# The beginning of layer 3 in a four-layer graph kernel: four groups of nodes between the last chunks of hop 2, residual and factor in one product, roots from bits

## The chip, the cores and the metric

The kernel runs on 1 core of one Trainium2 chip, as one launch. The metric is the device time in microseconds (us), as a median of runs. The profile is of one further execution of the program. In its lines PE is TensorE (PEld its weight loads), DVE is VectorE, ACT is ScalarE, POOL is GpSimd, and SPq is the queue of SyncE, which here issues nearly all transfers. A line such as L386 is line 386 of the kernel as it is before the change.

## The reference, cut to what matters

Four layers work on x (3327 nodes of 64 features) and one adjacency matrix adj (3327 x 3327); after each, the layer's input is added and a layernorm taken. Layers 2 and 3 are touched here:

```python
def _L2_gnn_ref(user_embs, adj, W):
    x = user_embs
    for k in range(2):                     # two hops
        agg = adj @ x
        x = jnp.tanh(jnp.concatenate([agg, x], axis=1) @ W[k])
    return x
def _L3_gnn_ref(input, adj, weight, bias):
    support = input @ weight
    mask = (adj != 0).astype(support.dtype)
    rank = jnp.cumsum(mask, axis=1)
    deg = rank[:, -1:]
    k = jnp.minimum(deg, 100.0)
    pos = rank - (deg - k)
    w = mask * jnp.where(pos > 0, 0.5 ** (k - pos), 0.0)
    return w @ support + bias
...
x = _layernorm(x + _L2_gnn_ref(x, adj, L2_gnn_W), axis=-1)
x = _layernorm(x + _L3_gnn_ref(x, adj, L3_gnn_weight, L3_gnn_bias), axis=-1)
```

Layer 3 gives each neighbour a weight that halves with every further neighbour that comes after it in its row. So it needs a count along the row, and products with weights that the count makes.

## The kernel before, in words

**Tiling.** The nodes are padded to 3328, 26 blocks of 128. The matrix comes transposed, so a block of 128 rows of `in_adjT` holds all edges that come from 128 nodes: 128 partitions x 3328 values, 1664 KB. A feature-major tensor such as `hT` is 128 x 1664: the 64 features of the first half of the nodes on 64 partitions, those of the second half on the other 64. It is cut into 4 chunks of 416 columns (`CPH`, `CW`).

**A hop of layer 2** (`for k in range(2)` in `layers`) adds 26 blocks into four accumulators in PSUM, one per chunk, each a tile of its own (`acc`, pool `l2a`). `add(c, jb)` (L386) does chunk c of block jb: two float32 products, one for each half, side by side on 64 columns of TensorE each. `top` and `bottom` (L344, L374, L377) multiply the node features with the two halves of W. Six blocks stay in SBUF: 25 to 22 (tiles `kept`, pool `early`) and 21, 20 (pool `late`). Six more are left over from the hop before (`ready`). Hop 2 streams the other 14 through two buffers `bt` and four buffers `at` (L204): a load is issued when the block that was in its buffer has been added. In what follows these 14 are s0 to s13, and the 26 blocks of hop 2 stand at places 0 to 25. Before the change places 0 to 5 are the left-over blocks, places 6, 11, 16 and 21 are the kept blocks 25 to 22, and the streamed blocks stand between them, s12 and s13 at places 22 and 23. The kept blocks 20 and 21 are last, chunk by chunk, so that each chunk can go through its tanh (L453, on ACT) while the next is added:

```python
                for c in range(CPH) if k == 0 else reversed(range(CPH)):
                    for jb in stay[-2:]:
                        add(c, jb, jb == stay[-1])
                    nc.scalar.activation(nxt[:, c * CW : (c + 1) * CW], acc[c], AF.Tanh)
```

After the second streamed block of hop 2, six masks (L326, DVE) are made from the six kept blocks, for the first six steps of layer 3.

**The beginning of layer 3** follows hop 2. `residual` turns h back to node-major and centers it in one product (L529), adds x2, squares and sums (L534, L537, L538). `scaled` takes roots with ACT's Sqrt and a Newton step (L231 to L238) and scales (L546). `turned` transposes x3 (L553, L557), and `factor` multiplies it by the weight matrix (L563) and splits the product into three bfloat16 parts (L569, L570, L571 and, on POOL, L572). These work on groups of 1, 4, 4 and 4 column blocks. Between them stand the first counting steps, `counts(0)` to `counts(2)`.

**The main loop** does 52 steps, 26 blocks for each half of the target nodes. Step q does for c = 0, 1: `advance` (L468; two products with `rest`, two with `tri`, into the count tiles `cnt`) and `products` of the step three before (L614; and every third step a group of 12 smaller ones, L627). Before a count tile can move on it must be read: `read` (L484 on ACT for c = 0, L482 on DVE for c = 1) turns its bits into weights `w`. DVE also makes the mask of the step three ahead from a half block `ah`, of which four are in flight (L324). Between the halves, `sums_out` (L643 on ACT, L644 on DVE) takes the first half's sums out of PSUM, and `half_out` (L653 to L679) does bias, residual and layernorm.

**What sets the order.** Every engine works through its own queue in order. TensorE's queue is in the order of the code throughout. In the two hops and the main loop DVE's and ACT's queues are too (`manual_schedule`); in the beginning of layer 3 a scheduler orders these two. Waits between engines are put in by the framework, by tiles.

Of the kernel before, what the change touches and what calls it, by code (L numbers as in the profile page):

```python
# [10 lines left out]
F32 = mybir.dt.float32  # L11
# [55 lines left out]
STEP = float(2**7)  # L67


@with_exitstack  # L70
def kernel(
# [65 lines left out]
    w3_dg = const.tile([P, P], F32, name="w3_dg")  # L137
# [39 lines left out]
    center = const.tile([P, P], F32, name="center")  # L177
# [120 lines left out]
    def layers(ctx, x2, kept, ready, ahead_ctx, strm):  # L298
# [52 lines left out]
        x3 = xpool.tile([P, NB, D], F32, tag="x", name="x3")  # L351
        hT = cols.tile([P, HALF], F32, tag="hT", name="hT_0")
        with tc.tile_pool(
            name="l2p", bufs=2, space=PSUM, reuse_waits="tile"
        ) as l2p, tc.tile_pool(
            name="l2a", bufs=CPH, space=PSUM, reuse_waits="tile"
        ) as l2a, tc.manual_schedule(
            engines={mybir.EngineType.DVE, mybir.EngineType.Activation}
        ):
            for k in range(2):  # L360
                hw = lj
                nxt = cols.tile([P, HALF], F32, tag="hT", name=f"hT_{k + 1}")
                acc = [l2a.tile([P, CW], F32, tag="acc", name=f"acc2_{k}_{c}") for c in range(CPH)]
# [30 lines left out]

                stay = list(kept)
                others = [jb for jb in range(NB) if jb not in kept and jb not in ready]
                share = -(-len(others) // (len(stay) - 2))
                order = list(ready)
                for i, jb in enumerate(stay[:-2]):
                    order += [jb] + others[i * share : (i + 1) * share]  # L400
                blocks = {**ready, **kept}

                if k == 0:
# [14 lines left out]
                    for c in range(CPH):  # L418
                        bottom(c)

# [29 lines left out]
                for c in range(CPH) if k == 0 else reversed(range(CPH)):  # L450
                    for jb in stay[-2:]:
                        add(c, jb, jb == stay[-1])
                    nc.scalar.activation(nxt[:, c * CW : (c + 1) * CW], acc[c], AF.Tanh)  # L453

# [18 lines left out]
        def read(q):  # L473
            if q >= len(steps):
                return
            h, jb = steps[q]
            for c in range(2):
                w = l3w.tile(
                    [P, 2, CW], BF16, tag=f"w{c}", bufs=LEAD + GROUP + 2, name=f"w_{h}_{jb}_{c}"
                )  # L480
                if c:
                    nc.vector.tensor_scalar(w.bitcast(I16), cnt[c], 0.0, None, ALU.max)  # L482
                else:
                    nc.scalar.activation(w.bitcast(I16), cnt[c], AF.Relu)  # L484
                ws[q, c] = w
# [10 lines left out]
        def rsqrt_of(v, w):  # L496

            nc.vector.tensor_scalar(v, v, 1.0 / D, LN_EPS, ALU.mult, ALU.add)
            return rsqrt(v, "ln", w)

        def spread(v, n):
# [8 lines left out]
        xT = cols.tile([P, HALF], F32, tag="hT", name="xT_3")  # L510
        s12 = l3n.tile([P, NB, 2, D], BF16, name="s12")
        s3 = l3n.tile([P, NB, D], BF16, name="s3")
        rr = lj
        l3w = ctx.enter_context(tc.tile_pool(name="l3w", bufs=2, reuse_waits="tile"))
        l3c = ctx.enter_context(
            tc.tile_pool(name="l3c", bufs=1, space=PSUM, reuse_waits="tile")
        )
        cnt = [l3c.tile([P, 2, 512], F32, name=f"cnt_{c}")[:, :, :CW] for c in range(2)]

        with tc.tile_pool(name="l3t", bufs=4, space=PSUM, reuse_waits="tile") as l3t:  # L520

            def ps(name):
                return l3t.tile([P, 4 * P], F32, tag="ps", name=name)

            def residual(g, n):

                pr = ps(f"pr_h2_{g}")
                for c in range(n):
                    nc.tensor.matmul(  # L529
                        pr[:, c * P : (c + 1) * P], hT[:, (g + c) * P : (g + c + 1) * P], center,  # L530
                        start=True, stop=True,
                    )
                sl = slice(2 * g, 2 * (g + n))
                nc.vector.tensor_tensor(  # L534
                    hid[:, sl], pr[:, : n * P].rearrange("p (n d) -> p n d", d=D), x2[:, sl], ALU.add
                )
                nc.scalar.activation(sq[:, sl], hid[:, sl], AF.Square)  # L537
                nc.vector.tensor_reduce(var[:, sl], sq[:, sl], axis=AX.X, op=ALU.add)  # L538

            def scaled(part):  # L540
                sl = slice(2 * part[-1][0], 2 * (part[0][0] + part[0][1]))
                r = rsqrt_of(var[:, sl], sl.stop - sl.start)
                for g, n in part:
                    s = slice(2 * g, 2 * (g + n))
                    o = s.start - sl.start
                    nc.vector.tensor_tensor(  # L546
                        x3[:, s], hid[:, s], spread(r[:, o : o + 2 * n], 2 * n), ALU.mult
                    )

            def turned(g, n, copy):  # L550
                pt = ps(f"pt_x3_{g}")
                for c in range(n):
                    nc.tensor.transpose(  # L553
                        pt[:, c * P : (c + 1) * P],
                        by_half(x3)[:, g + c].rearrange("p h d -> p (h d)"), ident,
                    )
                copy(xT[:, g * P : (g + n) * P], pt[:, : n * P])  # L557

            def factor(g, n):

                pn = ps(f"pn_l3_{g}")
                for c in range(n):
                    nc.tensor.matmul(  # L563
                        pn[:, c * P : (c + 1) * P], xT[:, (g + c) * P : (g + c + 1) * P], w3_dg,
                        start=True, stop=True,
                    )
                pn = pn[:, : n * P].rearrange("p (n d) -> p n d", d=D)
                sl = slice(2 * g, 2 * (g + n))
                nc.scalar.copy(s12[:, sl, 0, :], pn)  # L569
                nc.vector.tensor_tensor(rr[:, sl], pn, s12[:, sl, 0, :], ALU.subtract)  # L570
                nc.scalar.copy(s12[:, sl, 1, :], rr[:, sl])  # L571
                nc.gpsimd.tensor_tensor(s3[:, sl], rr[:, sl], s12[:, sl, 1, :], ALU.subtract)  # L572

            def counts(q):
                read(q)
                for c in range(2):
                    advance(c, q)

            last, second = fours[:1:-1], fours[1::-1]
            for g, n in last + second:  # L580
                residual(g, n)
            scaled(last)
            scaled(second)
            for c in range(2):
                count(c, tri, 0, True)
            counts(0)
            turned(*last[0], nc.scalar.copy)
            turned(*last[1], nc.vector.tensor_copy)
            counts(1)
            factor(*last[0])  # L590
            factor(*last[1])
            turned(*second[0], nc.scalar.copy)
            turned(*second[1], nc.vector.tensor_copy)
            counts(2)
            factor(*second[0])
            factor(*second[1])

# [85 lines left out]
        with tc.manual_schedule(engines={mybir.EngineType.DVE, mybir.EngineType.Activation}):  # L683
            for q in range(LEAD, len(steps) + LEAD + 1):
                read(q)
                masks(q + AHEAD)
                p = q - LEAD if q < NB + LEAD else q - LEAD - 1
                for c in range(2):
                    if q < len(steps):
                        advance(c, q)  # L690
                    if q != NB + LEAD:
                        products(p, c)
                if q == NB + LEAD - 1:
                    accT = sums_out(0)
                if q == NB + LEAD:
                    first_out = half_out(0, accT)
                if first_out is not None:
                    next(first_out, None)
# [17 lines left out]
    with tc.tile_pool(name="l1", bufs=1) as l1:  # L716
# [811 lines left out]

        n_below = nc.values_load(flag[0:1, 0:1])
        with tc.If(n_below == 0) as norms:  # L1530
            with ExitStack() as arm:
                x2 = xpool.tile([P, NB, D], F32, tag="x", name="x2")
                with tc.tile_pool(name="n1m", bufs=1) as n1m:
                    mT = n1m.tile([P, HALF], F32, name="mT")
                    sq_e = n1m.tile([P, 12, D], F32, name="sq_e")
                    t_e = n1m.tile([P, 12], F32, name="t_e")

                    xm = x2.rearrange("p n d -> p (n d)")[:, : 3 * CW]
                    near_sphere(mT, xm, sq_e, t_e)
                    blocks = blocks_ahead(arm)  # L1540
                    near_end(mT, xm, sq_e, t_e, x2)
                layers(x2, *blocks)
        with norms.Else():
            with ExitStack() as arm:
                x1 = xc
                x2 = xpool.tile([P, NB, D], F32, tag="x", name="x2_any")
# [6 lines left out]
                layers(x2, *blocks)  # L1553
# [31 lines left out]
```

## Time and profile before

| | us |
|---|---|
| median of 3 runs | 577.2 |
| the runs | 579.83, 574.63, 577.20 |
| the profiled execution, whole | 574.9 |
| its span in the profile | 573.2 |
| PE, DVE, ACT, POOL busy in the span | 529.3, 361.6, 275.0, 216.4 |
| mean granted TensorE clock | 0.985 |
| transfers | 145.26 MB, 253 GB/s over the span |

The profiled execution is 1.7 us longer than its span. Layer 3 with its beginning takes the last 165 us of the span. PE's busy time says that PE is occupied, not that it is at its peak: matmuls overlap, and their ends are modelled. A line of the timeline gives the start, the time taken, engine, source line, operation, tiles, the number of merged instructions, and in brackets how long the engine was idle before it and what ended that.

### The profile page before, as it was taken

To read this page: it belongs to the slowest core of one execution; us is meant where nothing else is said; L and a number is where in the kernel's file an instruction comes from. 1 tells how busy PE (TensorE), PEld (TensorE's weight loads), DVE (VectorE), ACT (ScalarE), POOL (GpSimd) and SP (SyncE) were. 2 spreads that over 40 slices of the span, in tenths; PEclk is the share of its full clock that TensorE was granted. 3 is DMA by queue.
4 is the path that set the end of the run, shared out by engine and by line. 5 is a ranking of instruction groups with operands and counts; after the bars stand their busy time and mean duration, and the time that the engine had idled before them with its cause. 6 is when DMAs were issued, how large, how long until landed. Compare 5 with 4: busy or idle time off the path is not lost.

```text
span 573.2 us, 7492 instructions
## 1 busy us (share of the span) xinstructions
PE 529.3 (92%) x2864; PEld 226.3 (39%) x2864; DVE 361.6 (63%) x510; ACT 275.0 (48%) x327; POOL 216.4 (38%) x134
## 2 busy tenths in 40 slices
PE   8899989999999999699999999999879999899992
PEld 5522222222222224254444444433455555555542
DVE  7899999999999998920000010300487787698733
ACT  4999999998999997330000100000453333333320
POOL 3799999999999998100000000000020000000000
PEclk9999999999999999989999999999999999999996
DMA  8977675650766653999999049996618995689701
GB/s 294 369 257 223 214 231 193 236 180 3 237 210 215 232 180 123 396 428 423 426 426 396 5 176 424 373 406 289 236 64 274 330 339 192 235 266 355 247 1 35
DMA packets 34020, 145.26 MB, mean 253 GB/s; under 512 B 10269, under 2 KB 11959, under 8 KB 28855
## 3 DMA queue, kind: packets, MB, share of 16 engines
q1 hardware_dynamic: 32295, 144.27, 68.4%
q10 hardware_dynamic: 1680, 0.43, 0.3%
q8 instruction: 24, 0.39, 0.3%
q14 instruction: 21, 0.17, 0.1%
HBM read 143.23 MB, written 0.87 MB: 251 GB/s over the span
## 4 chain that ended last, share of the span: by engine, by line
PE 63%; DVE 20%; ACT 9%; issue 3%; DMA 3%; DVEq 0%; POOL 0%; POOLq 0%; ACTq 0%
PE acc L386 24%; PE pq L910 12%; DVE v L931 12%; PE cnt L468 11%; PE acc L614 5%; ACT sg L886 3%; PE acc L627 3%; ACT pq L923 2%; DVE a L922 2%; DMA at_l<-in_adjT 2%; DVE w L482 2%; PE pn_l L344 1%; PE pr_o L653 1%; PE acc L377 1%; DVE mask L326 1%
## 5 line engine op out<-in xcount | busy, mean ns | idle before, releaser
L897 POOL TENSOR_TENSOR u<-sg,at 128x832 f32<-128x832 f32 x88 | 169.8, 1957 | 3.2 <-ACT sg L886 2.7
L910 PE MATMUL pq<-riT,ljT 64*128 64x416 f32 x416 | 100.3, 560 | 15.2 <-DVE v L931 6.3
L922 DVE SCALAR_TENSOR_TENSOR a<-pq,dl,u 128x832 f32<-128x832 f32 x104 | 111.9, 1077 | 3.0 <-PE pq L910 2.9
L923 ACT ACTIVATE pq<-pq,al,gas 128x832 f32<-128x832 f32 x104 | 104.9, 1010 | 15.2 <-DVE a L922 14.2
L931 DVE SCALAR_TENSOR_TENSOR v<-pq,a 128x832 f32<-128x832 f32 x104 | 105.7, 1016 | 1.1 <-ACT pq L923 0.8
L943 PE MATMUL acc<-v,xv 128*64 128x416 f32 x416 | 95.4, 538 | 0.1
L386 PE MATMUL acc<-at_l,lj 128*64 128x416 f32 x480 | 86.5, 514 | 1.0 <-DMA at_l<-in_adjT 1.0
L886 ACT ACTIVATE sg<-lb,rb 128x1664 f32<-128x1664 f32 (+1 forms) x53 | 87.3, 1647 | 0.1
L484 ACT ACTIVATE w<-cnt 128x832 int16<-128x832 f32 x52 | 44.8, 862 | 72.9 <-PE cnt L468 72.8
L453 ACT ACTIVATE hT<-acc 128x416 f32<-128x416 f32 x8 | 4.1, 517 | 149.4 <-PE acc L386 149.4
L572 POOL TENSOR_TENSOR s<-lj,s 128x512 bf16<-128x512 f32 (+1 forms) x4 | 3.9, 977 | 182.8 <-ACT s L571 182.8
L482 DVE TENSOR_SCALAR w<-cnt 128x832 int16<-128x832 f32 x52 | 53.2, 1024 | 26.3 <-PE cnt L468 25.0
L910 PEld LDWEIGHTS pq<-riT,ljT 64*128 64x128 f32 x416 | 31.6, 185 | 88.3 <-DVE v L931 83.0
L374 DVE COPY lj<-pn_l 128x384 f32<-128x384 f32 (+2 forms) x8 | 4.3, 542 | 86.7 <-PE pn_l L344 86.7
L468 PE MATMUL cnt<-mask,rest 128*128 128x416 bf16 x200 | 51.7, 340 | 3.3 <-ACT w L484 2.5
L386 PEld LDWEIGHTS acc<-at_l,lj 128*64 128x64 f32 x480 | 34.1, 138 | 50.6 <-issue 47.9
L468 PE MATMUL cnt<-mask,tri 128*128 128x416 bf16 x208 | 53.4, 339 | 0.1
L614 PE MATMUL acc<-w,s 128*128 128x416 bf16 x208 | 52.3, 340 | 0.8 <-DVE lj L570 0.8
L943 PEld LDWEIGHTS acc<-v,xv 128*64 128x64 f32 x416 | 20.6, 135 | 61.0 <-issue 57.7
L326 DVE TENSOR_SCALAR mask<-ah 128x1664 bf16<-128x1664 f32 x42 | 43.4, 1033 | 0.0
L386 PE MATMUL acc<-kept,lj 128*64 128x416 f32 x192 | 35.2, 513 | 0.0
L897 POOL TENSOR_TENSOR u<-sg,kept 128x832 f32<-128x832 f32 x16 | 30.9, 1965 | 3.8 <-ACT sg L886 3.8
(266 smaller groups left out, 391.8 us busy)
## 6 DMA issues: line engine op xcount, KB each, us to landing
at_l<-in_adjT SPq DMA_DIRECT2D x26, 1664.0 KB, 12.3
at<-in_adjT SPq DMA_DIRECT2D x44, 832.0 KB, 4.9
ah<-in_adjT SPq DMA_DIRECT2D x42, 832.0 KB, 6.6
bt_l<-in_adjT SPq DMA_DIRECT2D x8, 1664.0 KB, 11.1
kept<-in_adjT SPq DMA_DIRECT2D x6, 1664.0 KB, 8.7
lb<-lf_rows SPq DMA_DIRECT2D x2, 384.0 KB, 4.5
ljT<-ljT SPq DMA_DIRECT2D x4, 128.0 KB, 6.4
out<-hid SPq DMA_DIRECT2D x2, 256.0 KB, 5.8
```

The source lines that it names most:

```text
L326: nc.vector.tensor_scalar(mask[q], at, 0.0, None, ALU.not_equal)
L386: nc.tensor.matmul(acc[c][h * D : (h + 1) * D, :], hw[:, slot(jb), :], blocks[jb][:, o : o + CW], start=c not in begun, stop=last, skip_gr ...
L468: nc.tensor.matmul(cnt[c][:, e, :], mat, mask[q][:, of], start=start, stop=(mat is tri), skip_group_check=True,)
L482: nc.vector.tensor_scalar(w.bitcast(I16), cnt[c], 0.0, None, ALU.max)
L614: nc.tensor.matmul(acc[h, c][:, e, :], s12[:, slot(jb)].rearrange("p t d -> p (t d)"), ws[q, c][:, e, :], start=first, stop=last,)
L886: nc.scalar.activation(sg[:, :, of], lbs[:, :, of], AF.Sigmoid, bias=rb[:, sl : sl + 1])
L897: nc.gpsimd.tensor_tensor(u, sg[:, :, of], at[:, :, of], ALU.mult)
L910: nc.tensor.matmul(pq[:, h, :], ljT[h != jb // NBH][rows, of], riT[rows, ch * CW : (ch + 1) * CW], start=True, stop=True,)
L922: stt(a_s[t], pqs[t], dl[:, one], us.pop(t), op0=ALU.add, op1=ALU.mult)
L923: nc.scalar.activation(pqs[t], pqs[t], AF.Square, bias=al[:, one], scale=gas[:, one])
L931: stt(w, pqs.pop(t), CUBIC_REST, a_s.pop(t), op0=ALU.add, op1=ALU.mult)
L943: nc.tensor.matmul(accs[cp, ci][h * D : (h + 1) * D, :], xv[:, slot(jb), :], w[:, h, :], start=(jb == order[0]), stop=(jb == order[-1]),)
```

## The change

- The accumulators of the hops are no longer four tiles but the two count tiles of layer 3: chunks 0 and 1 are the two halves of the tile `cnt_0`, chunks 2 and 3 those of `cnt_1`.
- x2 is transposed into the memory of an earlier tensor and stays (`x2T`). So h + x2 is added feature-major (`with_x2`), chunk by chunk, after the tanh.
- At the start of hop 1 one product and one copy on ACT (`pw_3`) put center x weight beside `center`. With both as one 128 x 256 operand (`both_m`) one product gives the centered residual and its product with the weights (`finish`); scaling both by the root comes after.
- Roots are made on DVE alone, from the bits of the number (`roots`, nine instructions), not with ACT's Sqrt.
- The nodes are taken in four groups A, B, C, E of 3, 3, 3 and 4 column blocks, and the work on them stands between the last chunks of hop 2, in an order written out for PE, DVE and ACT.
- Hop 2 keeps three blocks for its end (24, 23, 22), not two (20, 21); 20 and 21 come at places 6 and 12, 25 at place 18, s12 and s13 at places 21 and 22.
- Between the halves, the reads of the next step now stand ahead of `sums_out`.

```diff
+        x2T = x3.rearrange("p n d -> p (n d)")
+        hT = x2T
...
+        cnt = [l3c.tile([P, 2, 512], F32, name=f"cnt_{c}")[:, :, :CW] for c in range(2)]
+        acc = [cnt[c // 2][:, c % 2, :] for c in range(CPH)]
...
-                acc = [l2a.tile([P, CW], F32, tag="acc", name=f"acc2_{k}_{c}") for c in range(CPH)]
...
+                if k:
+                    stay.sort(key=lambda jb: jb >= NB - EARLY)
+                n_end = 3 if k else 2
+                stay, end = stay[:-n_end], stay[-n_end:]
...
+                    pw = l2p.tile([P, 4 * P], F32, tag="pt", name="pw_3")[:, :P]
+                    nc.tensor.matmul(pw, center, w3_dg, start=True, stop=True)
+                    nc.scalar.copy(w3_dg, pw)
...
+                def chunk_end(c):
+                    for jb in end:
+                        add(c, jb, jb == end[-1])
                     nc.scalar.activation(nxt[:, c * CW : (c + 1) * CW], acc[c], AF.Tanh)
...
+        parts = ((10, 3), (7, 3), (4, 3), (0, 4))
...
+        def with_x2(c):
+            of = slice(c * CW, (c + 1) * CW)
+            nc.vector.tensor_tensor(nxt[:, of], nxt[:, of], x2T[:, of], ALU.add)
+
+        def finish(l3t, i):
+            g, n = parts[i]
+            pt = l3t.tile([P, 4, 2 * P], F32, tag="both", name=f"both_{i}")
+            for k in range(n):
+                nc.tensor.matmul(
+                    pt[:, k, :], nxt[:, (g + k) * P : (g + k + 1) * P], both_m,
+                    start=True, stop=True,
+                )
...
+        def squares(i):
+            nc.scalar.activation(halves(sq[:, slots(i)]), both[i][0], AF.Square, scale=0.125)
+        def sums(i):
+            nc.vector.tensor_reduce(var[:, slots(i)], sq[:, slots(i)], axis=AX.X, op=ALU.add)
+        def roots(sl):
+            v, y, t, p = (t[:, sl] for t in (var, y_all, e_all, p_all))
+            tt, stt = nc.vector.tensor_tensor, nc.vector.scalar_tensor_tensor
+            nc.vector.tensor_scalar(v, v, LN_EPS, None, ALU.add)
+            nc.vector.tensor_scalar(
+                y.bitcast(I32), v.bitcast(I32), -0.5, ROOT_BITS, ALU.mult, ALU.add
+            )
+            tt(t, v, y, ALU.mult)
+            tt(t, t, y, ALU.mult)
+            stt(p, t, -10.0 / 3.0, t, op0=ALU.add, op1=ALU.mult)
+            stt(y, p, 5.0, y, op0=ALU.add, op1=ALU.mult)
+            tt(t, v, y, ALU.mult)
+            tt(t, t, y, ALU.mult)
+            stt(y, t, -3.0 / 0.140625, y, op0=ALU.add, op1=ALU.mult)
+        def scaled(i, src, dst):          # one scalar_tensor_tensor on DVE
...
+        def factor(i):      scaled(i, both[i][1], rr)
+        def x3_of(i):       scaled(i, both[i][0], x3)
+        def x3_later(i):    scaled(i, halves(x3[:, slots(i)]), x3)
+        def hid_out(i):     nc.scalar.copy(halves(x3[:, slots(i)]), both[i][0])
+        def first_part(i):  nc.scalar.copy(s12[:, slots(i), 0, :], rr[:, slots(i)])
+        def rest_of(i):     nc.vector.tensor_tensor(rr[:, sl], rr[:, sl], s12[:, sl, 0, :], ALU.subtract)
+        def other_parts(i):
+            nc.scalar.copy(s12[:, sl, 1, :], rr[:, sl])
+            nc.gpsimd.tensor_tensor(s3[:, sl], rr[:, sl], s12[:, sl, 1, :], ALU.subtract)
...
+            chunk_end(3); with_x2(3); chunk_end(2); with_x2(2); finish(l3t, A); squares(A)
+            chunk_end(1); sums(A); roots(slots(A)); factor(A); with_x2(1); finish(l3t, B)
+            squares(B); x3_of(A); sums(B); first_part(A); count(1, tri, 0, True); read(1, 0, False)
+            rest_of(A); chunk_end(0); roots(slots(B)); with_x2(0); other_parts(A); finish(l3t, C)
+            count(0, tri, 0, True); advance(1, 0); squares(C); read(0, 0, False); factor(B); x3_of(B)
+            first_part(B); sums(C); finish(l3t, E); hid_out(C); advance(0, 0); rest_of(B)
+            read(1, 1, True); squares(E); hid_out(E); advance(1, 1); read(0, 1, False); other_parts(B)
+            sums(E); advance(0, 1); roots(slice(0, 2 * sum(parts[C]))); read(1, 2, False)
+            advance(1, 2); read(0, 2, False); advance(0, 2); factor(C); factor(E)
...
+        with_step = {
+            LEAD: lambda: (first_part(C), rest_of(C), other_parts(C)),
+            LEAD + 1: lambda: (first_part(E), rest_of(E), other_parts(E)),
+            LEAD + 2: lambda: x3_later(C),
+            LEAD + 3: lambda: x3_later(E),
+        }
+        for q in range(LEAD, len(steps) + LEAD + 1):
+            read(0, q, False)
+            read(1, q, True)
+            if q == NB + LEAD:
+                accT = sums_out(0)
+            masks(q + AHEAD)
+            with_step.pop(q, lambda: None)()
```

(The calls of the beginning, each on a line of its own in the code, are put together here, and short functions are put on one line.)

## The prediction

> **What bounds the kernel now.** First the chain that ended last, by engine:
>
> ```profile
> PE 63%; DVE 20%; ACT 9%; issue 3%; DMA 3%; DVEq 0%; POOL 0%; POOLq 0%; ACTq 0%
> ```
>
> The change touches the time from hop 1's end on. There I cut two windows: the beginning of layer 3, from the end of hop 2 to step 6 of the main loop, and the main loop after it. Columns: us, then busy time and count of PE, PEld, DVE, ACT, POOL, then clock, DMA share, GB/s.
>
> ```profile
> 407.70:434.04 26.34, 21.15 (x143) 14.23 (x142) 21.91 (x41) 14.54 (x25) 3.86 (x4) 1.00 0.44 157
> 434.04:456.90 22.86, 22.86 (x147) 12.12 (x146) 17.66 (x19) 7.77 (x9) 0.00 (x0) 1.00 0.93 327
> ```
>
> In the main loop PE never waits, and three steps take 7.61 us. So whatever brings step 6 forward brings the end forward by as much. In the beginning PE waits 5.2 us; more could come only from work removed. I use the start of step 6 (434.04) as the mark.
>
> Next the timeline of hop 2's end, transfers included:
>
> ```profile
> 361.82 25.47 SPq L204 DMA_DIRECT2D at_l<-in_adjT  x8
> 381.16 8.71 PE L386 MATMUL acc<-at_l,lj 128*64 128x416 f32 x48
> 390.86 3.01 PE L386 MATMUL acc<-at_l,lj 128*64 128x416 f32 x16 [0.98 <-DMA at_l<-in_adjT]
> 396.49 5.76 PE L386 MATMUL acc<-at_l,lj 128*64 128x416 f32 x32
> 402.08 1.22 PE L386 MATMUL acc<-kept,lj 128*64 128x416 f32 x6
> ```
>
> A block is 16 records, 2.79 us on PE, but 4.0 us for the DMA: s9 landed at 382.85, s11 at 390.81, s13 at 398.81 in the trace. PE waited for s11, and s13 came 0.5 us ahead of its use at 399.28. So hop 2's end hangs on the transfers; the reader should keep this in mind when blocks change places.
>
> Then hop 1's end, and the turn between layer 3's halves:
>
> ```profile
> 321.35 5.76 PE L386 MATMUL acc<-kept,lj 128*64 128x416 f32 x32
> 322.96 0.52 ACT L453 ACTIVATE hT<-acc 128x416 f32<-128x416 f32 x1 [68.11 <-PE acc L386]
> 324.36 0.52 ACT L453 ACTIVATE hT<-acc 128x416 f32<-128x416 f32 x1 [0.88 <-PE acc L386]
> ```
> ```profile
> 491.62 0.88 PE L614 MATMUL acc<-w,s 128*128 128x416 bf16 x4
> 492.18 0.95 ACT L643 ACTIVATE accT<-acc,b_sb 128x832 f32<-128x832 f32 x1 [3.39 <-PE acc L614]
> 493.04 0.85 ACT L484 ACTIVATE w<-cnt 128x832 int16<-128x832 f32 x1
> 493.94 0.51 PE L468 MATMUL cnt<-mask,rest 128*128 128x416 bf16 x2 [1.44 <-ACT w L484]
> ```
>
> In the first, PE runs through 32 records without a gap while ACT makes the tanh of a chunk that is done. In the second, the read that PE needs (L484) stands in ACT's queue behind a copy (L643) that waits for PE's last products.
>
> **Term 1, the turn: -1.6.** Those products end at 492.33 (four at 0.175 from 491.62), and PE goes on at 493.94: 1.61 us lost. With the reads ahead of `sums_out`, ACT can read at 490.0 and DVE by 491.9, so PE goes straight on; its two advances (1.4) last until 493.73, and the copies (492.18 + 0.95, 492.54 + 1.08) are then done, so the output products don't wait either. Behind the copies on DVE stands only a mask for three steps on. Bounds: 0 to 1.6; I take all of it.
>
> Sqrt's table load moves from the beginning to this half's root, behind the read of step 32:
>
> ```profile
> 413.41 1.28 ACT L231 ACT_TABLE_LOAD   x1
> 505.08 0.21 ACT L231 ACTIVATE ln_r<-v_out 128x13 f32<-128x13 f32 x1 [2.35 <-DVE v_out L498]
> ```
>
> It takes 1.28 us, and ACT sat idle there for 2.35 us until DVE delivered: nothing, and up to 1.28 if the load waits too. The Trainium skill ("ScalarE: Activation LUTs", "What ACT_TABLE_LOAD costs") puts a switch at about 2.66 us, a drain included; that would pass the idle time by an estimated 0.3 us. In the trace Sqrt starts 11 ns after the load, so I leave the drain out.
>
> **Term 2, the end of hop 1: +1.6, of which 1.5 comes back.** Two chunks now share a tile, and the built program makes PE's second chunk wait for the tanh of the first. From a chunk's last slot (322.75) to tanh is 0.21, tanh 0.52, and on to PE 0.05 (L453 to L529 at 408.45): about 0.8 us, for chunk 1 and again for chunk 3. Hop 2's stream starts 1.6 later, since its first load (336.11) waits for a left-over block to be added. The cover: s8 takes the buffer of s4, which is added one place earlier. s8 landed 5.46 us after s7, not 4.0, because it was issued only at 370.20, 3.1 us before s7 landed. Issued 2.79 earlier in step with the rest, it should follow at 4.0 and win 1.46. s13 then lands at 398.81 + 1.6 - 1.46 = 398.95. If this fails, the term is 1.5 dearer. `pw_3` adds a 128-column product (0.22) and a copy; in hop 1 PE waits for transfers, so 0 to 0.2, and I take 0.
>
> **Term 3, the beginning: +0.3.** s13 is now at place 22, due one block earlier, so PE waits for it and ends it at 398.95 + 0.05 + 2.79 = 401.8; call that 0. Before, the closing chunks began at 402.08, and step 6 came 31.96 later. Now the walk is this.
>
> PE's work up to step 6: four chunks of three blocks, 24 x 0.349 = 8.4; `finish`, 13 products of 256 columns, from L377's 0.349 per record of 416 columns 0.43 each, 5.6; 26 pairs of counting products at 0.349 (L468), 9.1; six pairs of L614, 2.1; one group of L627, 1.1; seven changes between 64- and 128-column work at 0.1 (485.50 to 485.77 before L627), 0.7. Together 27.0. What goes away is the work of L529, L553 and L563, 39 products at 0.22, 8.7; what is added is 5.6 and the third kept block, which is only moved.
>
> PE's waits, in order, from rows on DVE and ACT. Small DVE steps that depend on each other start every 0.21 us (505.60, 505.81, 506.02 in the trace); wide ones of 384 elements take 0.55 to 0.6 (between L538's 0.29 for 128 and 0.68 for 512); a copy or square of 384 on ACT 0.5 (L537: 0.31 and 0.63).
> - 0.8: chunk 2 waits for tanh of chunk 3, as in term 2. Chunk 0 doesn't, group A stands between.
> - 0.6: group E's product waits at 14.9 for `x3_of(B)`, which frees its PSUM buffer. DVE is then in one unbroken run from `sums(A)` at 7.2: eighteen root steps (3.7) and eight wide instructions (4.6), to 15.4.
> - 0.8: after 18.6 for `read(0, 1)`, behind square and copy of E on ACT (0.6 each).
> - 0.6: two reads of 0.86 in a row on ACT, where PE has 0.7 of work between.
> - 1.1: at 22.1 for `read(0, 3)`; PE has nothing else, and the round trip is 0.23 + 0.86 + 0.05.
> - 0.3 and 1.5: in steps 4 and 5 the casts of C and E stand ahead of the reads on ACT. The second cast of E waits for `rest_of(E)`, which on DVE is queued behind a mask of 1.02.
>
> Sum 5.7. Step 6 starts at 27.0 + 5.7 = 32.7 (with the overlaps of some 0.1 carried through, 32.55), or 401.8 + 32.55 = 434.35: 0.3 later than before. So the 8.7 us removed go to the moved block (2.8), `finish` and new waits. DMA: the first `ah` loads are issued from 401.8 on, three of them earlier than before (407.88); their masks are due from 423 on. Nothing there. `x3_later` is DVE work in steps 5 and 6, 0.6 and 0.7, under a DVE that is 77% busy.
>
> **Sum.** -1.6 + 0 + 0.3 = -1.3 against the profiled execution's 574.9: 573.6. The median of the runs is 2.3 above that execution, so in such a median 577.2 - 1.3 = 575.9. One per cent, 5.8 us, is about what a measurement of this kernel can tell from no change.
>
> **Rivals.**
> *The beginning overlaps fully.* The new waits of term 3 vanish, apart from the shared tile's 0.8: 5.7 - 0.8 = 4.9 more, so 575.9 - 4.9 = 571.0. For it: DVE and ACT are idle in hop 2's end. Against: the waits come from queues in a fixed order, with durations that the rows give.
> *DVE's chain becomes the bound (slower than before).* There are 27 dependent root steps. If each took what the reciprocal takes (0.24 at L232, and 0.035 to the next), that is 27 x 0.065 = 1.8, and 0.1 more on each of eight wide ones with PSUM source (L534's 0.69 for 512 against my 0.6) 0.8: -1.3 + 2.6, 578.5. It decides from 1.3 us in all, 0.05 a step. Against it: L234 to L238 show 0.17.
> *The stream doesn't win back its delay:* +1.5, 577.4, no change. For it: 4.0 us is the floor of a block, and PE sets when buffers come free.
>
> **How the numbers follow.** Forecast, no change within 1%: 0.65, own range 572.5 to 578.5 with the runs' spread of 2.6 to each side in part. Stream late: 0.13, also within 1%. Full overlap: 0.12, which with its neighbours is the chance of faster by over 1%. DVE's chain: 0.10, of which the far end is slower by over 1%; other mishaps make up what little it lacks, so 0.10. Faster 0.12, same 0.78, slower 0.10. The range: below, full overlap, 571.0, less a little; above, 575.9 + 1.5 + 2.6 = 580.0.
>
> **What would show it.** Two idle times of 0.8 on PE in hop 1's end, released by L453's successor; s8 landing 4.0 after s7; PE waiting for s12 and s13; the eight waits above in the beginning, the longest 1.5 in step 5; no wait at the turn; a table load near 502 in ACT's idle time. I am wrong if step 6 comes more than 2 us from its old time, or if the loop after it no longer takes 7.61 for three steps.

## The result and the profile after

The changed kernel takes 576.94 us (median of 12 runs, 575.70 to 577.93), the kernel before in the same runs 577.09 (574.61 to 579.83). The ratio is 1.0002 with a 95% interval of 0.9985 to 1.0019, that is -0.9 to +1.1 us: no change. Forecast were 575.9, no change, and a range from a little under 571.0 to 580.0. The chain that ended last has hardly moved, and the loop has its old pace: the second window below starts at step 6 and again takes 22.86 us with PE busy throughout.

The chain of the changed kernel, by engine:

```profile
PE 63%; DVE 19%; ACT 8%; DMA 4%; issue 4%; POOL 0%; DVEq 0%; POOLq 0%
```

Its windows (us, then busy time and count of PE, PEld, DVE, ACT, POOL, then clock, DMA share, GB/s); the first runs from hop 2's closing chunks to step 6:

```profile
404.50:437.26 32.76, 28.66 (x153) 14.47 (x149) 24.10 (x55) 15.68 (x27) 4.10 (x4) 1.00 0.47 164
437.26:460.12 22.86, 22.86 (x147) 12.13 (x146) 18.24 (x20) 7.77 (x9) 0.00 (x0) 1.00 0.91 315
```

And what PE waited for from hop 1's end to step 6 (total, times, longest):

```profile
PE cnt L491 <- ACT w L506: 3.5, 5, 1.0
PE cnt L395 <- DMA at_l<-in_adjT: 2.4, 3, 1.0
PE cnt L395 <- ACT hT L471: 1.9, 3, 0.6
```

The kernel is best compared by stretches between events that both have. The times are from the two profiled executions, in us:

| stretch | before | after | change | forecast |
|---|---|---|---|---|
| hop 1's first transpose to its first product with the weights | 2.14 | 3.05 | +0.91 | 0 |
| from there to hop 1's first tanh | 77.65 | 77.82 | +0.17 | 0 |
| first tanh to hop 2's first product with the weights | 4.07 | 5.75 | +1.68 | +1.6 |
| from there to the closing chunks of hop 2 | 75.04 | 73.96 | -1.08 | -1.9 |
| closing chunks to step 6 | 31.96 | 32.75 | +0.79 | +0.6 |
| step 6 to the last products of the first half | 58.12 | 58.12 | 0 | 0 |
| from there to the first output product (the turn) | 3.19 | 1.58 | -1.61 | -1.6 |
| from there to the end | 77.83 | 78.04 | +0.21 | 0 |
| sum | 330.00 | 331.08 | +1.08 | -1.3 |

(The forecast of the fourth row is 401.8 - 402.08 = -0.28 for the start of the closing chunks, less the 1.6 of the row above.) What lies before hop 1 is left out: in the profiles that follow, hop 1's first transpose comes anywhere from 243.2 to 245.1 us with the same code ahead of it. In the second row the profiles of the changed kernel's own code spread from 77.8 to 78.8 (TensorE's clock has a part in that, see the second experiment), and in the last row all profiles from 77.8 to 78.4, so no difference between the two kernels is read from them alone.

The two waits that term 2 forecast for hop 1's end, in the timeline:

```profile
324.79 0.52 ACT L471 ACTIVATE hT<-cnt 128x416 f32<-128x416 f32 x1 [61.24 <-PE cnt L395]
325.36 3.01 PE L395 MATMUL cnt<-kept,lj 128*64 128x416 f32 x16 [0.62 <-ACT hT L471]
328.43 0.52 ACT L471 ACTIVATE hT<-cnt 128x416 f32<-128x416 f32 x1 [0.88 <-PE cnt L395]
329.00 1.62 PE L395 MATMUL cnt<-kept,lj 128*64 128x416 f32 x8 [0.62 <-ACT hT L471]
```

The second chunk of each tile stands behind the tanh of the first: 0.62 of idle time by the modelled ends, 0.84 in the length of the stretch, twice.

The turn, where PE goes from the last products (L689) into the next step without a gap, while ACT copies the sums (L718):

```profile
494.84 0.88 PE L689 MATMUL acc<-w,s 128*128 128x416 bf16 x4
495.40 0.95 ACT L718 ACTIVATE accT<-acc,b_sb 128x832 f32<-128x832 f32 x1 [1.28 <-PE acc L689]
495.55 0.52 PE L491 MATMUL cnt<-mask,rest 128*128 128x416 bf16 x2
496.96 3.01 PE L728 MATMUL pr_o<-center,accT 128*128 128x64 f32 x26
```

And Sqrt's table load, which fits into ACT's idle time as forecast: after it ACT still waits 0.98 us for DVE.

```profile
504.42 1.28 ACT L236 ACT_TABLE_LOAD   x1
506.69 0.22 ACT L236 ACTIVATE ln_r<-v_out 128x13 f32<-128x13 f32 x1 [0.98 <-DVE v_out L520]
```

### The profile page after: what moved, and what is told of

Its sections match the earlier page's. It is cut to its first block, busy times and chain, and to the rows that moved or that the text cites. A ratio compares the mean times of both kernels' runs of the same rounds, so it can differ in the third digit from the quotient of the medians.

```text
span 575.0 us, 7445 instructions
## 1 busy us (share of the span) xinstructions
PE 529.6 (92%) x2827; PEld 223.8 (39%) x2827; DVE 364.4 (63%) x525; ACT 276.5 (48%) x328; POOL 217.1 (38%) x134
## 4 chain that ended last, share of the span: by engine, by line
PE 63%; DVE 19%; ACT 8%; DMA 4%; issue 4%; POOL 0%; DVEq 0%; POOLq 0%
PE cnt L395 22%; PE pq L993 12%; DVE v L1014 12%; PE cnt L491 11%; PE acc L689 6%; DMA at_l<-in_adjT 4%; ACT sg L969 3%; PE acc L702 3%; ACT pq L1006 2%; DVE a L1005 2%; PE pn_l L349 1%; PE both L558 1%; PE pr_o L728 1%; PE cnt L386 1%; PE idle L829 1%
## 5 line engine op out<-in xcount | busy, mean ns | idle before, releaser
L395 PE MATMUL cnt<-at_l,lj 128*64 128x416 f32 x480 | 86.5, 513 | 2.4 <-DMA at_l<-in_adjT 2.4
L506 ACT ACTIVATE w<-cnt 128x832 int16<-128x832 f32 x54 | 46.5, 863 | 71.1 <-PE cnt L491 71.1
L471 ACT ACTIVATE hT<-cnt 128x416 f32<-128x416 f32 x8 | 4.1, 517 | 146.3 <-PE cnt L395 146.3
L618 POOL TENSOR_TENSOR s<-sq,s 128x384 bf16<-128x384 f32 (+1 forms) x4 | 4.1, 1024 | 186.2 <-ACT s L617 186.2
L504 DVE TENSOR_SCALAR w<-cnt 128x832 int16<-128x832 f32 x50 | 51.2, 1023 | 24.7 <-PE cnt L491 24.0
L395 PEld LDWEIGHTS cnt<-at_l,lj 128*64 128x64 f32 x480 | 34.0, 137 | 51.9 <-issue 46.5
L689 PE MATMUL acc<-w,s 128*128 128x416 bf16 x208 | 52.3, 339 | 0.0
L395 PE MATMUL cnt<-kept,lj 128*64 128x416 f32 x192 | 36.2, 515 | 1.9 <-ACT hT L471 1.9
```

Of the source, the lines that this page charges most:

```text
L395: nc.tensor.matmul(acc[c][h * D : (h + 1) * D, :], hw[:, slot(jb), :], blocks[jb][:, o : o + CW], start=c not in begun, stop=last, skip_gr ...
L689: nc.tensor.matmul(acc[h, c][:, e, :], s12[:, slot(jb)].rearrange("p t d -> p (t d)"), ws[q, c][:, e, :], start=first, stop=last,)
```

## The experiments

Each run has its own profile. "To step 6" means the fifth row of the table.

**The turn, undone and alone** (e1, e8). In the changed kernel the copies go back ahead of the reads; in the kernel before only the reads are moved.

```diff
+            if q == NB + LEAD:
+                accT = sums_out(0)
             read(0, q, False)
             read(1, q, True)
-            if q == NB + LEAD:
-                accT = sums_out(0)
```

> The changed kernel with one part undone: at the turn the copies of the sums (sums_out) stand ahead of the reads again. If term 1 is right, the whole 1.6 us comes back: from the last high products (L689) to the first output product it takes 2.12 us in the changed kernel and 3.73 in the kernel before; expected here 3.7, with PE waiting 1.4 for the read on ACT, and everything behind it 1.6 later. If the rival holds (the time was lost there anyway, in another wait), 2.1 and no difference at the end.

> The kernel before with one part of the change alone: the reads of the next step ahead of the copies of the sums at the turn. If term 1 doesn't depend on the rest: from the last high products to the first output product 1.6 us instead of 3.2, and the time 1.6 less, 0.997 of before. Rival: no gain, because the copies then come too late for the output products (3.2 again).

Undone: 3.19 us again in that row, 578.55 us, ratio 1.0033 (1.0019 to 1.0046), and PE waits for the read:

```profile
497.33 0.86 ACT L506 ACTIVATE w<-cnt 128x832 int16<-128x832 f32 x1
498.24 0.51 PE L491 MATMUL cnt<-mask,rest 128*128 128x416 bf16 x2 [1.45 <-ACT w L506]
```

(The expectation gave 2.12 and 3.73 for this row, counted from the first of the last products; the table counts from the last of them, 1.58 and 3.19.) Alone: 1.58, ratio 0.9975 (0.9954 to 0.9996). Term 1 is right, and independent of the rest.

**Where the 0.9 us at hop 1's beginning comes from** (e2). The timeline of the changed kernel there:

```profile
243.92 0.52 PE L339 MATMUL pt_x<-ident,x 128*128 128x128 f32 x3 [0.57 <-DVE x L1406]
245.75 0.74 DVE L1406 TENSOR_TENSOR x<-pm,bx 128x384 f32<-128x384 f32 x2
246.55 0.63 PE L339 MATMUL pt_x<-ident,x 128*128 128x128 f32 x3 [2.11 <-DVE x L1406]
246.97 1.49 PE L349 MATMUL pn_l<-w_dg,xc 128*128 128x128 f32 x6
```

The second group of transposes starts when layer 1's last sums (L1406, which read the tiles `pm` in PSUM) end at 246.49, though its own three blocks of x2 were done earlier.

```diff
-            tc.tile_pool(name="l3c", bufs=1, space=PSUM, reuse_waits="tile")
+            tc.tile_pool(name="l3c", bufs=1, space=PSUM, side="right", reuse_waits="tile")
```

> The changed kernel with the two count tiles put at the other end of PSUM, so that hop 1's work tiles lie in the lower four banks, as before the change. In the changed kernel the second group of transposes waits 2.1 us for layer 1's last sums, and it takes 3.05 us from the first transpose to the first product with the weights, against 2.14 before. If that wait is on the PSUM banks that layer 1 still reads, 2.1 to 2.2 us here, and hop 1's first tanh, hop 2's end and the end of the kernel come 0.9 earlier. Rival: it comes from x2's new place in SBUF (the copies on ACT), then still 3.05. Second rival: hop 1 waits for transfers and hides it, then 2.1 at its beginning, and nothing at its end.

With the count tiles at the other end of PSUM the second group starts at once:

```profile
243.84 0.52 PE L339 MATMUL pt_x<-ident,x 128*128 128x128 f32 x3 [0.57 <-DVE x L1406]
244.68 0.55 PE L339 MATMUL pt_x<-ident,x 128*128 128x128 f32 x3 [0.32 <-DVE x L1406]
245.98 0.94 PE L349 MATMUL pn_l<-w_dg,xc 128*128 128x128 f32 x6 [0.76 <-ACT xc L343]
```

The row is 2.14 again, and the time 574.64, ratio 0.9973 (0.9955 to 0.9990). x2's place in SBUF is as in the changed kernel, so that rival is out. The second rival, that hop 1 hides the 0.9, is out too. From the first transpose to hop 1's first tanh it takes 80.9 to 82.1 us in the eight profiles with the wait, and 78.5 to 79.4 in the three of the changed kernel without it (this run and the two at the end of this section). So the tiles' new place costs more than the 0.9 of the row, and a part of the rest is TensorE's clock. Windows of the changed kernel and of this run, columns as above:

```profile
247.00:250.00 3.00, 3.00 (x16) 3.00 (x15) 0.00 (x0) 1.43 (x3) 0.00 (x0) 0.50 1.00 426
```
```profile
247.00:250.00 3.00, 3.00 (x23) 1.65 (x23) 0.56 (x1) 0.81 (x2) 0.00 (x0) 1.00 1.02 435
```

In all eight profiles with the wait the clock is halved here for 3.4 us (in three of them for 6.8; these three take 82.0 to 82.1, the other five 80.9), and in none of the three without it. The kernel before has this stretch of 3.4 us in its own profile, without the wait, and not in the run with the turn alone; so the wait isn't the only thing that brings it on.

**Hop 1's closing order** (e3).

```diff
-                for c in range(CPH):
+                for c in (0, 2, 1, 3):
                     chunk_end(c)
```

> The changed kernel with hop 1's closing chunks in the order 0, 2, 1, 3, so that neighbours in time lie in different tiles. The two waits of 0.62 (0.8 of PE's time each) at hop 1's end should go: from the first tanh to hop 2's first product with the weights 4.1 to 4.2 us, not 5.75. If transfers set hop 2's end and each load waits for a block that is added, hop 2's stream, its closing chunks, step 6 and the end all come 1.6 earlier. Rival: the stream has its own pace and gives the gain back: PE waits 1.6 more for s8 to s13, and the closing chunks start as in the changed kernel, 0 in all.

The row is 4.07, as before the change. Hop 2 takes 73.59 us, no more than the other profiles of its order (73.23 to 74.21), so the stream starts 1.7 earlier and gives nothing back: 574.74, ratio 0.9972 (0.9958 to 0.9985). The expected 4.1 to 4.2 was a little too much.

**Hop 2's order** (e5).

```diff
+                if k:
+                    order = list(ready) + others[:6] + stay[:1] + others[6:9] + stay[1:2]
+                    order += others[9:12] + stay[2:] + others[12:]
```

> The changed kernel with hop 2's blocks in another order: s0 to s5 directly behind the left-over blocks, kept blocks 20, 21 and 25 at places 12, 16 and 20, so that s6 to s9, which wait for the buffers of s2 to s5, are issued 2.8 us earlier. In the changed kernel s6 lands 5.3 us after s5, s8 4.8 after s7, where 4.0 is the pace of a full queue: 2.1 us of the stream are lost. If the late issue costs that, all six land 4.0 after the one before, and the closing chunks start 1.1 to 2.2 us earlier, counted from hop 2's first product with the weights (73.2 to 74.1 us in five profiles of this order, so 71.5 to 72.7). Rival: the landing rows are uneven for another reason (the memory or other queues), then no change, 73.2 to 74.1.

All blocks from s6 on land 4.0 us after the one before. In the changed kernel s6 took 5.33, issued 2.1 us ahead of s5's landing; here it is issued 4.7 ahead and takes 4.00. Hop 2 takes 71.97 us, 2.0 less than in the changed kernel's profile, and PE waits for one block instead of three:

```profile
PE cnt L395 <- DMA at_l<-in_adjT: 0.6, 1, 0.6
```

The time is 575.63, ratio 0.9980 (0.9962 to 0.9998). Eight profiles of the changed kernel's own order give 73.23 to 74.21, on average 73.7; two of the order before 75.04 and 74.35. So the change wins about 1.0 here on average, and one profile is good to some 0.5 us.

**The casts ahead of the reads** (e4). In the changed kernel step 4 begins like this:

```profile
427.92 1.01 DVE L331 TENSOR_SCALAR mask<-ah 128x1664 bf16<-128x1664 f32 x1
428.85 0.55 DVE L613 TENSOR_TENSOR sq<-sq,s 128x384 f32<-128x384 f32 x1
429.43 0.51 ACT L617 CAST s<-sq 128x384 bf16<-128x384 f32 x1 [1.46 <-DVE sq L613]
429.85 0.86 ACT L506 ACTIVATE w<-cnt 128x832 int16<-128x832 f32 x1
430.76 0.51 PE L491 MATMUL cnt<-mask,rest 128*128 128x416 bf16 x2 [0.87 <-ACT w L506]
```

ACT is idle for 1.46 us, and in the last 0.9 of it the count tile is ready to be read (in the run below ACT waits 0.55 for it and no longer): a cast is ahead in its queue, which waits for DVE's subtraction (L613), which waits behind a mask.

```diff
-            LEAD: lambda: (first_part(C), rest_of(C), other_parts(C)),
-            LEAD + 1: lambda: (first_part(E), rest_of(E), other_parts(E)),
-            LEAD + 2: lambda: x3_later(C),
-            LEAD + 3: lambda: x3_later(E),
+            LEAD: lambda: (first_part(C), rest_of(C)),
+            LEAD + 1: lambda: other_parts(C),
+            LEAD + 2: lambda: (first_part(E), rest_of(E)),
+            LEAD + 3: lambda: other_parts(E),
+            LEAD + 4: lambda: x3_later(C),
+            LEAD + 5: lambda: x3_later(E),
```

> The changed kernel with the casts of groups C and E in the main loop spread over steps 3 to 6, each second cast one step behind its subtraction, and x3_later two steps later. If the casts ahead of the reads on ACT cause the waits at steps 4 and 5 (0.87 and 0.85 in the list of waits, 1.03 and 1.02 counted from start to start), both go, and from the closing chunks to step 6 it takes 32.76 - 2.0 = 30.7 us; I worked out 30.9 to 31.2 beforehand, since DVE may give back a little. Rival: the DVE reads behind masks and subtractions take their place, then at most 1.0 is won.

To step 6 it takes 30.72 us, 2.03 less. The read now starts when PE has advanced the tile, and PE goes on without a wait:

```profile
427.48 0.52 PE L689 MATMUL acc<-w,s 128*128 128x416 bf16 x2
427.68 0.86 ACT L506 ACTIVATE w<-cnt 128x832 int16<-128x832 f32 x1 [0.55 <-PE cnt L491]
428.88 0.52 PE L491 MATMUL cnt<-mask,rest 128*128 128x416 bf16 x2
```

573.99 us, ratio 0.9956 (0.9940 to 0.9972).

**Is DVE's chain at its limit?** (e6, e7, e11). In the changed kernel `x3_of(B)` ends at 419.85 and group E's product starts at 420.00, straight after PE's work ahead of it. To see how much room there is, one run gives PE less to wait for, one makes the roots longer.

```diff
             chunk_end(3)
+            for jb in end[:1]:
+                add(1, jb)
             with_x2(3)
...
-            chunk_end(1)
+            chunk_end(1, end[1:])
```
```diff
-            tt(t, v, y, ALU.mult)
+            for _ in range(7):
+                tt(t, v, y, ALU.mult)
             tt(t, t, y, ALU.mult)
```

> The changed kernel with chunk 1's first kept block added between chunks 3 and 2 of hop 2, 0.7 us of PE work in place of the wait for tanh (0.62 in the list of waits, 0.79 from start to start). The wait goes by any theory. If the chain of small instructions on DVE holds up group E (in the changed kernel E's product starts at 420.00, x3_of(B) ends at 419.85), E's product starts where it did, PE waits 0.7 there, and from the closing chunks to step 6 it still takes 32.7 to 32.8 us. Rival: PE is the bound there, then 32.0.

> The changed kernel with the first product of each root formed seven times over instead of once: six more instructions of 0.20 us in each of the three root chains (groups A, B, and C with E). If DVE's chain stands on the path without slack, as in the run that covers chunk 2, group E's product comes 2.4 us later, and from the closing chunks to step 6 it takes 35.2 to 35.6 us. Rival: PE's waits for the reads cover most of it, then at most 33.8.

Both came out dearer than expected: 33.36 us to step 6 in the first (577.55, ratio 1.0013, 0.9993 to 1.0033), 37.09 in the second (582.19, ratio 1.0092, 1.0063 to 1.0122). In the first the wait for tanh is gone, and E's product waits 1.22 us for DVE instead. Half of that is one small instruction of the chain:

```profile
418.66 0.92 POOL L618 TENSOR_TENSOR s<-sq,s 128x384 bf16<-128x384 f32 x1 [175.16 <-ACT s L617]
418.83 0.77 DVE L585 TENSOR_TENSOR root_e<-root_e,root_y 128x6 f32<-128x6 f32 x1
421.38 1.97 PE L558 MATMUL both<-both_m,hT 128*128 128x256 f32 x8 [1.22 <-DVE xc L591]
```

It takes 0.77 us, where its neighbours take 0.17, and ends (419.60) when POOL's subtraction does (419.58). In the run with long roots the seven products of B's chain take 2.05 us, not 1.36, across POOL's 419.00 to 419.91; E's product waits 3.01 where 2.4 were worked out. The rest of its 4.3 us is lost in steps 3 and 4, where the longer chain of C and E reaches: a new wait of 0.47, and 1.49 instead of 0.87. To test POOL's part, its subtraction was moved out of the way in the run that covers chunk 2:

```diff
             with_x2(0)
-            other_parts(A)
...
             x3_of(B)
             first_part(B)
+            other_parts(A)
```

> The run that covers chunk 2, with group A's cast on ACT and subtraction on POOL (L617, L618) moved behind first_part(B), past the root chain of B. There an instruction of the chain took 0.77 us, not 0.17, and it ended as POOL's subtraction did. If POOL holds DVE up, no instruction of B's chain takes over 0.25 here, group E's product waits 0.6 for DVE instead of 1.22, and from the closing chunks to step 6 it takes 32.7 to 32.8, not 33.36. Rival: it was something else (a wait on PE or ACT), then 33.4 again.

```profile
419.18 0.17 DVE L585 TENSOR_TENSOR root_e<-root_e,root_y 128x6 f32<-128x6 f32 x1
421.13 1.97 PE L558 MATMUL both<-both_m,hT 128*128 128x256 f32 x8 [0.62 <-DVE xc L591]
421.62 1.06 POOL L618 TENSOR_TENSOR s<-sq,s 128x384 bf16<-128x384 f32 x1 [176.77 <-ACT s L617]
```

All instructions of the chain take 0.17, the wait is 0.62, and it is 32.77 us to step 6, as in the changed kernel (a single execution, 577.98 us). So DVE's chain has no room here: what PE is spared ahead of it, it loses behind it.

**The four edits that won time, together** (e9), and two more to shorten DVE's chain (e10): the cover for chunk 2 as above, and

```diff
-            x3_of(B)
...
             read(1, 0, False)
+            hid_out(B)
             rest_of(A)
...
+            LEAD + 6: lambda: x3_later(B),
```

> The changed kernel with the four edits that won time together: count tiles at the other end of PSUM (0.9 us), hop 1's closing chunks in the order 0, 2, 1, 3 (1.7), hop 2's new order (2.0), the casts spread over steps 3 to 6 (2.0). If they add up, 6.6 us less than the changed kernel: 576.9 - 6.6 = 570.3, 0.989 of the kernel before, with 2.1, 4.1, 72.0 and 30.7 us in the four stretches (to the first product with the weights, hop 1's end, hop 2, closing chunks to step 6). Rival: hop 2's stream takes back what hop 1's end gives, since in the new order its loads no longer wait for PE; then 73.7 in hop 2 and 572.

> The four edits, and two more in the beginning: chunk 1's first kept block between chunks 3 and 2, and group B's x3 copied unscaled out of PSUM by ACT (as for C and E) and scaled in step 9, so that DVE's chain ahead of group E's product is shorter by one instruction of 0.47 us. If DVE's chain decides, E's product comes 0.5 earlier, and from the closing chunks to step 6 it takes 30.2 us, not 30.7: 569.8. Rival: DVE waits again for POOL in that place, as in the run that covers chunk 2 (an instruction of 0.17 took 0.77 there), then 30.7 or a little more.

Together they take 570.63 us, 0.9891 of the kernel before (0.9867 to 0.9915): the gains add up as far as an interval of 2.8 us can tell. By their ratios the four runs are 7.3 us below the changed kernel in sum; together they are 6.4 below it. The rows are 2.14, 4.07, 72.33 and 30.72. What PE still waits for from hop 1's end to step 6 (lines are numbered three higher here):

```profile
PE cnt L494 <- ACT w L509: 1.8, 3, 1.0
PE cnt L395 <- DMA at_l<-in_adjT: 1.0, 2, 0.5
PE cnt L395 <- ACT hT L474: 0.6, 1, 0.6
```

The two further edits bring nothing: 30.80 us to step 6, 570.30, ratio 0.9893 (0.9866 to 0.9919). The rival was right: at 412.34 an instruction of B's chain takes 0.76 us beside POOL's subtraction, and E's product waits 0.66 for `factor(B)`.

## Why the prediction was right, point by point

**No change** was right, and so was the outline of the reason: a gain of 1.6 at the turn, set against waits at hop 1's end and in the beginning. But the prediction's own sign of being wrong has come: step 6 was not to move by more than 2 us, and it starts at 437.26, not 434.04. Of these 3.2 us, 0.75 lie ahead of hop 1's first transpose and 2.47 behind it, where +0.3 was forecast. The rows of the table add up to +1.08 instead of -1.3, mainly because 0.91 was left out and 0.8 of hop 2 didn't come back. That 575.9 is only 1.0 below the median is therefore luck in part: the profile of before that the terms were read from was quicker than most executions of that kernel (see the last point).

**Term 1** (the turn, -1.6) is exact, and the table load cost nothing, as said.

**Term 2.** The 1.6 at hop 1's end was 1.68. The stream was to win back 1.46 at s8, and PE a further 0.42; the row won 1.08 in this profile and about 1.0 on average. The failed step is the landing of s8: 4.84 us after s7, not 4.0. In eight profiles of this order (the changed kernel and the experiments that leave hop 2 alone) it took 4.00 to 5.45, twice 4.00, though it was issued 5.5 to 6.9 us ahead of s7's landing; in the two of the order before 5.46 and 5.20. So an earlier issue helps, but not each time. The block that comes too late is s6, which took 4.84 to 6.57 in those eight; the three profiles with the new order have 4.0 for every block. I had corrected one gap of two. Why s8 is still uneven behind a late s6 stays open. The third rival (the stream isn't won back) was about half true: 0.8 to 0.9 of the 1.9 in that row didn't come.

**Term 3** (the beginning, +0.3): 32.55 from the closing chunks to step 6 were worked out, 32.75 measured. Here are the waits, from start to start, forecast and measured: chunk 2 on tanh 0.8 and 0.79; E's product on `x3_of(B)` 0.6 and none; `read(0, 1)` 0.8 and 0.69; two reads 0.6 and 0.46; `read(0, 3)` 1.1 and 1.11; steps 4 and 5 0.3 and 1.03, 1.5 and 1.02. Sum 5.7 and 5.1. (The prediction speaks of eight waits; its list has these seven.) The work was 0.65 more than the 27.0 forecast, above all in `finish` (1.40 to 1.49 for three blocks, from 0.43 per block I had 1.29), and so PE reached group E's product later, when DVE was just done. In step 4 the cast waits for a subtraction behind a mask; I had seen that for group E only. Of the size of these terms, then, four were off (E's product 0.6 and step 5 0.5 too high, step 4 0.7 and PE's work 0.65 too low). They nearly cancel, so that the sum came out within 0.2 is luck; four of the seven waits stand where they were forecast, within 0.15.

**What was missing** is the first row of the table, +0.91. I asked what shares the accumulators' new tiles, but not which banks the other tiles of hop 1 get when the count tiles take the first four. It gave PE's second group of transposes a new wait of 2.11 us. To hop 1's first tanh the run that undoes it is 1.5 us quicker than the changed kernel's profile (79.4 against 80.9), part of it by the clock.

**Rivals.** Full overlap (571.0) fell: the waits are there, in the queues' order. Of the 4.9 us, 2.0 come back when the casts change places; the reads' own round trips (0.69, 0.46 and 1.11) remain in every run. DVE's chain as the bound (578.5) didn't come, since the small steps start every 0.20 us and not every 0.27. But the chain has next to no slack: of the 2.4 us that the run with long roots puts ahead of group E's product, about 2.3 come out as a wait there (3.01, less the 0.69 that the chain loses beside POOL).

**Profile and median.** By the profiles the changed kernel is 1.1 us slower over the stretches of the table; by the medians it is 0.15 faster, by the ratio -0.9 to +1.1. Both hold if the profile of before was a lucky one: its 574.9 lay 2.2 below the median, while the changed kernel's profiled execution (576.84) lies at its own. The other runs say that it was. Of 73 more executions of the kernel before, measured beside the experiments, two took less than 574.9. Each is listed with its mean clock: the 33 at 0.985 or more have a median of 575.6 us, the 14 at 0.980 or less one of 577.9. The changed kernel's twelve lie between 0.982 and 0.988, and the eight of them at 0.985 or more have a median of 576.8, so at a like clock it is some 1.2 us slower, as the profiles say; the two groups weren't measured side by side, which makes this an indication. One way in which a lower clock costs time is shown by the run with the turn alone. Its code is that of before up to the turn, but to step 6 it took 33.49 us, not 31.96. Windows of that run and of before, at the same place behind the 2.3 us in which PE waits for the first x3 (the clock is the third column from the end):

```profile
417.50:420.50 3.00, 3.00 (x12) 1.71 (x11) 1.77 (x4) 0.86 (x1) 0.00 (x0) 0.52 0.00 0
```
```profile
418.50:421.50 3.00, 3.00 (x24) 2.38 (x22) 2.83 (x5) 1.26 (x3) 0.00 (x0) 1.00 0.00 0
```

The granted clock is 0.52 in the one and 1.00 in the other, with the same code and the same idle time (2.28 and 2.27). The changed kernel has no idle time on PE above 1 us from there to step 6, and none of its profiles shows a lower clock in this stretch. How often the kernel before loses these 1.5 us, and how often it loses time at hop 1's beginning, isn't known; two profiles don't tell.

## What to carry to other kernels

A wait in a hand-written order is often in the queue and not in the data: ACT stood idle for 1.46 us, 0.9 of it with a read ready to go, behind a cast that waited for DVE. Ask of each instruction what it stands ahead of, and put those that nobody needs soon behind the ones that the bounding engine waits for; here that won 2.0 us. When tiles are shared or pools change places, look for the waits of the work that lies next to them as well: in PSUM a new neighbour cost 0.9 us where it lay (1.5 by hop 1's first tanh), and two chunks in one tile 1.7, which another order of the chunks gave back. Hold a forecast against its own signs of being wrong as well as against the time: here the time was right, and step 6 was not.

## What the hardware showed that was not expected

DVE stands still beside POOL. Small instructions with two inputs in SBUF, which take 0.17, took 0.76 to 0.87 us wherever they met POOL's subtraction (fourteen places in the profiles), and ended within 0.03 us of it; masks (1.02) took 1.3 to 1.9 there and ended 0.88 after it. Instructions of 384 elements with one input in PSUM kept their 0.55 beside it in the changed kernel (L591 at 418.84 and 419.30), and there POOL's, which began while an addition of two inputs in SBUF was running on DVE (L551 at 418.33, until 418.91), took 1.12, not 0.91. The Trainium skill ("SBUF — State Buffer", "SBUF: two separate sides") states a lock on a port that the two engines share, held for a whole instruction, against DVE operations with two inputs in SBUF or in a mode that uses both ports; the rows agree for the small instructions.

TensorE's clock can halve after a short pause: it stood at half for 3.4 us after 2.28 us without work, in one execution out of two. In every trace here the falls lie whole multiples of 3.41 us apart. Laid on that grid, the pause of the run with the turn alone fills most of one stretch (PE busy for 0.93 of 3.41 us, then the fall at 417.60), and the equal pause of before is cut in two (1.7 and 1.9 us busy, no fall). Ahead of the nine falls at hop 1's beginning PE was busy for 0.8 to 1.8 us of the stretch. That isn't the whole rule: in the run with long roots a stretch with 1.5 us (from 419.0) was followed by no fall. The Trainium skill ("TensorE: Matmul & The Clock Gate", "What's actually happening") speaks of a free-running window of 3.4 us, which fits that one of two equal pauses was hit, and of a whole idle window for the clock to fall; here 2.28 us were enough.
